# A four-layer conditional residual stack on one core: setup as movable stages with products of zeros, the last pair's adapter batch by batch with filler products, and tables of their own for two pairs at each end

## The chip, the core and the metric

The kernel runs on 1 core of one Trainium2 chip. The metric is the device time of one execution in microseconds (us); the kernel before takes 1067.29 us, the median of 3 runs (1067.28 to 1068.83). The engines are PE (TensorE: matrix products and transposes), DVE (VectorE), ACT (ScalarE), POOL (GpSimd) and SP (SyncE, which here issues nearly all DMAs). Each engine works through its own queue of instructions in order.

## What is computed

32 batches of 256 x 256 numbers go through four layers, each added to its input:

```python
x = x + attention(x, f, len)      # 16 heads of 16
x = x + adapter(x, language)
x = x + linear(x, subject)
x = x + pooling(x, prompt_type)
```

- Attention: queries are from `f + b_self`, keys and values from `x` (keys with `b_prev`), masked by a length for each batch, and each query also has its own key and value from `f`. In the reference:

```python
score_prev = einsum('bhqd,bhkd->bhqk', q, k[:, :, :l1]) * SCALE
score_self = (q * k[:, :, l1:]).sum(-1, keepdims=True) * SCALE
score_prev = where(mask, score_prev, -inf)
weights = softmax(concatenate([score_prev, score_self], -1))
attn = einsum('bhqk,bhkd->bhqd', weights[..., :-1], v[:, :, :l1])
attn = attn + weights[..., -1:] * v[:, :, l1:]
return attn @ Wo + bo
```

- Adapter: `relu(x @ W1[language] + b1) @ W2[language] + b2`, added to x and normalised (layernorm) with gamma and beta of the language. 256 to 64 to 256 columns.
- Linear: `x @ W[subject].T + b[subject]`.
- Pooling: `scores = tanh(x @ W1 + b1) @ v`; each of 256 rows takes a softmax of the scores under one of three masks (up to the row, from the row, all but the row), weighs the rows of x with it and divides by the count.

All is in float32.

## The kernel before

Two batches make a pair, 16 pairs in all. The work on a pair is cut into some 110 stages: small functions that take the pair's number p and mostly the batch within the pair (i) and issue a few instructions each. Every stage has a time in a table: FIRST for pair 0, SLOTS for pairs 1 to 14, LAST for pair 15, and ONCE for what is done once. A pair's times are shifted by PERIOD = 16 for each pair. At the end of the program all stages of all pairs are sorted by time and called in that order, so the tables alone fix the order in every engine's queue (the scheduler is switched off by `tc.manual_schedule()`). A pair's times run from about -14 to 55, so that some four pairs are under way together: while the scores of one pair are computed, the adapter, the linear layer and the pooling of earlier ones are done, and the loads of later ones.

The stages that matter here, with the lines of the profile:

- Beginning. A fixed head loads lengths, biases, Wq and Wk, makes masks and constants (`cols`, `len_f`, `mcol`, `ones`; zeroed buffers `vpad`, `nmpad`, `epad` on POOL) and two tiny products (cols_ps L640). `setup_q`, `setup_k`, `setup_ks` (L684) each do four products of one column with a weight to get a projected bias, and `setup_k` also loads Wv, Wo and others on ACT's queue, `setup_ks` the ids on SP's. `setup_rest` makes `heads`, `vbc` and the constant xconst (L737). For pair 0 xT is loaded on ACT's queue, everything else on SP's.
- Attention. proj_q, proj_k, proj_ks (L937: qps, kps, ksps, two products of 512 columns each); self_values and proj_v (vs_ps, v_ps, L804); s1 (L1036: scores s, eight products into a tile of four PSUM banks, of which there is one), row_max (L1049 on DVE), max_T (L1065) and max_own (L1073), which put the row maximum into the q tile by a DMA; s2 (L1145: the scores again, transposed, into the same tile), exps (L1157 on ACT), av (L1167); av_blocks, sums, weighted, with_own (L1179 to L1199, DVE and POOL), att_T (L1206), out_proj (o_ps, L804).
- Adapter. x_bias (L892, POOL) adds xconst to x; x1_out (L1222), x1_T; hidden (L1251: h_ps), h_out (L1265 on ACT: hT), adapted (L1279: y_ps), each for both batches of a pair at once; y_out (L1290), norm_stats (L1298), norm_rstd (L1306 on POOL), norm_shift, norm (L1320 on ACT), x2_out (L1328 and L1329 on DVE: multiply by gamma into x1c, add into x1b), x2_T (L786: transposes into x2T_ps).
- Linear and pooling. subject (z_ps, L804), x2_bias (L1342 on POOL), x3_out; pool_hidden (L1362: t_ps), th_out (L1376 on ACT), both for two batches at once; pool_scores (L1384), pool_mask (L1394), pool_exp (L1405), pr_T (L786), pooled (p_ps, L804), store (L1433).

The helper `product` (L804) does v, vs, o, z and p: four products of 256 columns each. PSUM has one tile of four banks for scores, one bank for av, and three tiles of 128x512 (`g_tile`) in turn for everything else.

Of the kernel before, what the change touches and what calls it, by code (L numbers as in the profile page):

```python
# [16 lines left out]
P = 128  # L17
# [19 lines left out]
    (("setup_q",), -49.3857),  # L37
    (("setup_k",), -19.8446),
    (("setup_ks",), -6.186),
    (("setup_rest",), -3.7537),  # L40
    (("setup_tw_bias",), 1.524),
    (("setup_tw_load", 0), 2.5417),
    (("setup_tw", 0), 5.9494),
    (("setup_tw_load", 2), 10.3657),
    (("setup_tw_load", 1), 11.2065),
    (("setup_tw", 1), 11.7201),
    (("setup_tw", 2), 12.0733),
    (("setup_tw_load", 3), 15.02),
    (("setup_tw", 3), 15.4506),
    (("setup_tw_load", 5), 17.2034),  # L50
    (("setup_tw_load", 4), 17.9245),
    (("setup_tw", 4), 21.0263),
    (("setup_tw", 5), 23.7521),
    (("setup_tw_load", 6), 24.1631),
    (("setup_tw_load", 7), 24.4783),
    (("setup_tw", 6), 26.9562),
    (("setup_tw", 7), 28.331),
    (("setup_pool",), 28.3669),
# [4 lines left out]
    (("load_T", "xT"), -13.5215),  # L63
    (("load_T", "fT"), -10.3917),
    (("key_mask", 0), -9.9073),
    (("mask_keys", 0), -7.2255),
    (("key_mask", 1), -4.9533),
    (("proj_q", 0), -4.4466),
    (("mask_keys", 1), -3.9573),
    (("q_out", 0), -3.6777),  # L70
    (("proj_k", 0), -2.4273),
    (("k_out", 0, 1), -1.9747),
    (("self_values", 0), -1.5169),
    (("k_out", 0, 0), -1.1613),
    (("vs_blocks", 0), -0.0939),
    (("proj_k", 1), 0.1938),
    (("s1", 0, 0), 0.9084),
    (("k_out", 1, 0), 1.2453),
    (("row_max", 0, 0), 1.3039),
    (("proj_q", 1), 1.586),  # L80
    (("k_out", 1, 1), 3.0678),
    (("s1", 0, 1), 3.244),
    (("q_out", 1), 3.2483),
    (("proj_ks", 0), 3.5014),
    (("row_max", 0, 1), 3.5842),
    (("ks_out", 0), 4.797),
    (("proj_v", 0), 5.2874),
    (("s1", 0, 2), 5.6623),
    (("row_max", 0, 2), 5.7692),
    (("proj_ks", 1), 5.795),  # L90
    (("spread_q", 1, 1), 5.8634),
    (("ks_out", 1), 5.8758),
    (("spread_q", 1, 0), 5.9303),
    (("s1", 0, 3), 7.7652),
    (("row_max", 0, 3), 7.7705),
    (("proj_v", 1), 8.095),
    (("spread_q", 0, 1), 8.1965),
    (("v_out", 0), 8.4638),
    (("v_out", 1), 8.8903),
    (("load_x",), 9.0442),  # L100
    (("s1", 1, 0), 9.0718),
    (("spread_q", 0, 0), 9.4749),
    (("ones_rows", 0), 9.491),
    (("own",), 9.7621),
    (("row_max", 1, 0), 9.8401),
    (("own_out",), 9.9648),
    (("load_adapter", 1), 10.5636),
    (("max_T", 0), 10.8193),
    (("s1", 1, 1), 11.1319),
    (("max_own", 0), 11.2444),  # L110
    (("row_max", 1, 1), 11.6016),
    (("s2", 0, 0), 11.6887),
    (("exps", 0, 0), 12.3045),
    (("s1", 1, 2), 13.3127),
    (("row_max", 1, 2), 14.1015),
    (("s2", 0, 1), 14.1573),
    (("exps", 0, 1), 14.4065),
    (("s1", 1, 3), 14.948),
    (("av", 0, 1), 15.0649),
    (("av", 0, 0), 15.0931),  # L120
    (("row_max", 1, 3), 15.3191),
    (("own_exp", 0), 15.5608),
    (("max_T", 1), 15.661),
    (("max_own", 1), 15.664),
    (("s2", 0, 2), 16.0157),
    (("exps", 0, 2), 16.2354),
    (("ones_rows", 1), 16.6823),
    (("av_blocks", 0, 0), 18.0554),
    (("own_blocks", 0), 18.3788),
    (("s2", 0, 3), 18.4335),  # L130
    (("own_exp", 1), 18.607),
    (("weighted", 0), 18.6408),
    (("av", 0, 2), 18.8873),
    (("exps", 0, 3), 18.9415),
    (("sums", 0, 0), 19.5731),
    (("s2", 1, 0), 20.565),
    (("with_own", 0, 0), 21.02),
    (("exps", 1, 0), 21.4915),
    (("av", 0, 3), 21.9185),
    (("s2", 1, 1), 22.6692),  # L140
    (("self_values", 1), 22.7919),
    (("exps", 1, 1), 23.02),
    (("av_blocks", 0, 1), 23.1327),
    (("sums", 0, 1), 23.5444),
    (("vs_blocks", 1), 23.6805),
    (("with_own", 0, 1), 23.7081),
    (("av", 1, 0), 23.7805),
    (("x_bias",), 24.2529),
    (("s2", 1, 2), 24.3639),
    (("att_T", 0), 24.4799),  # L150
    (("out_proj", 0), 24.5865),
    (("exps", 1, 2), 24.8801),
    (("x1_out", 0), 24.9932),
    (("load_adapter", 0), 25.6776),
    (("own_blocks", 1), 25.9991),
    (("av", 1, 1), 26.0785),
    (("av_blocks", 1, 0), 26.4561),
    (("s2", 1, 3), 26.6748),
    (("exps", 1, 3), 26.6765),
    (("weighted", 1), 26.9644),  # L160
    (("av", 1, 3), 27.5753),
    (("av", 1, 2), 27.5808),
    (("load_subject",), 27.9373),
    (("x1_T", 0), 28.0348),
    (("sums", 1, 0), 28.1731),
    (("with_own", 1, 0), 28.187),
    (("av_blocks", 1, 1), 28.6458),
    (("sums", 1, 1), 28.6986),
    (("with_own", 1, 1), 28.8383),
    (("x1T_out", 0), 29.2985),  # L170
    (("att_T", 1), 29.737),
    (("x1_b2", 0), 29.7867),
    (("out_proj", 1), 30.1273),
    (("x1_out", 1), 30.1913),
    (("x1_T", 1), 32.2936),
    (("x1T_out", 1), 32.4643),
    (("x1_beta", 0), 32.9228),
    (("x1_beta", 1), 33.8118),
    (("hidden",), 34.6069),
    (("h_out",), 35.0271),  # L180
    (("x1_b2", 1), 35.3287),
    (("adapted",), 36.3452),
    (("y_out", 1), 36.5305),
    (("y_out", 0), 36.6375),
    (("norm_stats", 0), 37.1251),
    (("norm_stats", 1), 37.201),
    (("norm_rstd", 0), 37.246),
    (("norm_rstd", 1), 37.2713),
    (("norm_shift", 0), 37.4371),
    (("norm", 0), 38.2498),  # L190
    (("norm_shift", 1), 38.2508),
    (("x2_out", 0), 39.0757),
    (("x2_T", 0), 39.6396),
    (("norm", 1), 39.7894),
    (("x2_bias", 0), 40.0974),
    (("x2_out", 1), 40.1578),
    (("x2T_out", 0), 40.3738),
    (("x2_T", 1), 40.4639),
    (("load_pool",), 40.7288),
    (("x2T_out", 1), 41.1509),  # L200
    (("pool_hidden",), 41.4167),
    (("th_out",), 41.5067),
    (("pool_scores", 0), 42.2295),
    (("x2_bias", 1), 42.4414),
    (("pool_scores", 1), 42.6152),
    (("pool_mask", 0), 42.7126),
    (("subject", 0), 42.9261),
    (("x3_out", 0), 43.2303),
    (("pool_mask", 1), 43.6816),
    (("pool_exp", 0), 44.056),  # L210
    (("subject", 1), 44.2113),
    (("pool_exp", 1), 44.3238),
    (("x3_out", 1), 44.7583),
    (("pr_T", 0), 46.893),
    (("prT_out", 0), 47.2894),
    (("pr_T", 1), 47.5751),
    (("pool_factor", 1), 47.6166),
    (("pool_factor", 0), 47.9292),
    (("prT_out", 1), 48.0167),
    (("pooled", 0), 49.1393),  # L220
    (("store", 0), 50.5365),
    (("pooled", 1), 53.4761),
    (("store", 1), 54.4432),
# [4 lines left out]
    (("load_T", "xT"), -37.5523),  # L228
    (("key_mask", 0), -19.5291),
    (("mask_keys", 0), -13.821),  # L230
    (("key_mask", 1), -12.6569),
    (("load_T", "fT"), -9.8489),
    (("mask_keys", 1), -7.5382),
    (("proj_k", 0), -5.9091),
    (("k_out", 0, 1), -5.8806),
    (("proj_q", 0), -2.9721),
    (("k_out", 0, 0), -2.808),
    (("self_values", 0), -2.1146),
    (("q_out", 0), -1.6303),
    (("s1", 0, 0), -0.879),  # L240
    (("proj_k", 1), 0.1292),
    (("row_max", 0, 0), 0.8243),
    (("k_out", 1, 0), 0.9903),
    (("k_out", 1, 1), 1.4355),
    (("s1", 0, 1), 1.5728),
    (("proj_q", 1), 1.6701),
    (("spread_q", 0, 1), 2.6443),
    (("proj_ks", 0), 3.2664),
    (("row_max", 0, 1), 3.4033),
    (("q_out", 1), 3.476),  # L250
    (("s1", 0, 2), 3.7112),
    (("spread_q", 1, 1), 4.0254),
    (("proj_ks", 1), 4.6937),
    (("ks_out", 0), 5.0527),
    (("row_max", 0, 2), 5.6196),
    (("ks_out", 1), 5.8464),
    (("spread_q", 0, 0), 6.0284),
    (("vs_blocks", 0), 6.3593),
    (("s1", 0, 3), 7.2806),
    (("own",), 7.3892),  # L260
    (("proj_v", 0), 7.4415),
    (("row_max", 0, 3), 7.549),
    (("spread_q", 1, 0), 7.7204),
    (("s1", 1, 0), 7.7777),
    (("max_T", 0), 7.7783),
    (("own_out",), 10.1669),
# [290 lines left out]
def cond_resid_kernel(  # L557
# [41 lines left out]
    def g_tile(name):  # L599
        return ps_g.tile([P, 512], F32, tag="g", name=name)  # L600
# [943 lines left out]
```

## Time and profile before

| | |
|---|---|
| median of 3 runs | 1067.29 us |
| the profiled execution | 1068.81 us |
| its span | 1066.7 us |
| mean granted TensorE clock | 0.995 |
| DVE, ACT, POOL busy | 70%, 48%, 34% |
| PE busy in the first 10 us / the next 10 | 2.16 / 8.88 us |
| PE busy from 1040 to 1050 us / 1050 to the end | 5.15 / 11.92 us |
| granted clock in those two | 0.80 / 0.81 |
| time from one pair to the next (pairs 3 to 13) | 63.6 us |

A row of the profile reads: start, duration (both in us), engine, line, operation, output <- inputs, and in brackets how long the engine had stood idle before it and what released it. In a table of waits it is: engine, tile and line of the waiting instruction <- engine, tile and line of the one waited for: total us, times, longest. In a table of windows: the window's length, then busy time of PE, PEld (weight loads), DVE, ACT and POOL (with the number of instructions), the granted clock, the DMA share, GB/s.

### The profile page before, as it was taken

How to read it: one execution, taken by the hardware profiler on the slowest of the kernel's cores; microseconds unless marked ns; L12 is line 12 of the kernel's file. 1: busy time of each engine (PE TensorE's matmuls, PEld its weight loads, DVE VectorE, ACT ScalarE, POOL GpSimd, SP SyncE). 2: the span in 40 equal slices, each digit the busy share in tenths (PEclk: the TensorE clock that was granted, in tenths of full speed). 3: DMA queues.
4: the chain of work that ended last, by engine and by line, in shares of the span. 5: the costliest groups of instructions: out<-in, count | busy, mean ns of one | idle time of the engine just before them, and what ended most of it. 6: DMA issues, size and time to landing. Idle time of an engine off the chain costs nothing.

```text
span 1066.7 us, 20863 instructions
## 1 busy us (share of the span) xinstructions
PE 1029.1 (96%) x7912; PEld 591.9 (55%) x7912; DVE 750.7 (70%) x1239; ACT 514.1 (48%) x722; POOL 367.5 (34%) x489
## 2 busy tenths in 40 slices
PE   6999999999999999999999999999999999999996
PEld 4455555555555555555555555555555555555564
DVE  4757586767768687686767867686786867757764
ACT  1243454544545544545545545455455545455552
POOL 2022362432424244233332514243233333514541
PEclk9999999999999999999999999999999999999998
DMA  4223231321313132132311312222132311311222
GB/s 136 60 71 104 84 105 49 106 59 53 115 64 91 39 99 76 53 91 67 98 50 62 111 57 91 58 84 74 52 96 70 103 57 56 101 34 52 68 76 68
DMA packets 58985, 81.08 MB, mean 76 GB/s; under 512 B 7238, under 2 KB 40774, under 8 KB 58886
## 3 DMA queue, kind: packets, MB, share of 16 engines
q1 hardware_dynamic: 57782, 77.46, 24.4%
q10 hardware_dynamic: 864, 1.51, 0.6%
q8 instruction: 63, 1.03, 0.4%
q0 software_dynamic: 240, 0.79, 0.2%
q14 instruction: 36, 0.29, 0.1%
HBM read 68.45 MB, written 9.71 MB: 73 GB/s over the span
## 4 chain that ended last, share of the span: by engine, by line
PE 86%; DVE 9%; ACT 2%; POOL 1%; DMA 1%; issue 1%; SPq 0%; DVEq 0%; ACTq 0%
PE s L1036 13%; PE s L1145 11%; PE av L1167 10%; PE kps L937 6%; PE z_ps L804 5%; PE ksps L937 5%; PE o_ps L804 5%; PE qps L937 5%; PE p_ps L804 5%; PE vs_ps L804 5%; DVE nmpad L1049 4%; PE v_ps L804 3%; DVE x1c L1328 2%; PE t_ps L1362 2%; PE y_ps L1279 2%; PE x2T_ps L786 2%
## 5 line engine op out<-in xcount | busy, mean ns | idle before, releaser
L1157 ACT ACTIVATE e<-s 128x2048 f32<-128x2048 f32 x128 | 240.3, 1878 | 377.5 <-PE s L1145 377.5
L1049 DVE TENSOR_REDUCE nmpad<-s 128x8 f32<-128x2048 f32 x128 | 292.7, 2287 | 164.6 <-PE s L1036 164.6
L1036 PE MATMUL s<-k,qc 32*128 32x512 f32 x1024 | 146.0, 640 | 4.1 <-ACT e L1157 2.8
L1145 PE MATMUL s<-q,k 32*128 32x256 f32 x2048 | 146.7, 400 | 1.4 <-DVE nmpad L1049 1.2
L1132 POOL TENSOR_TENSOR vs<-vs,eown 128x256 f32<-128x256 f32 x64 | 38.9, 629 | 292.4 <-DVE eown L1097 292.4
L1167 PE MATMUL av<-e,vpad 128*32 128x256 f32 x2048 | 130.7, 383 | 0.0
L1145 PEld LDWEIGHTS s<-q,k 32*128 32x128 f32 x2048 | 92.5, 184 | 51.7 <-issue 20.6
L1167 PEld LDWEIGHTS av<-e,vpad 128*32 128x32 f32 x2048 | 57.8, 109 | 83.6 <-issue 42.5
L1198 POOL TENSOR_TENSOR vs<-bt,vs 128x256 f32<-128x256 f32 x64 | 46.9, 733 | 111.3 <-DVE bt L1179 111.3
L1199 POOL TENSOR_TENSOR vs<-vs,zs 128x256 f32<-128x256 f32 x64 | 40.3, 630 | 108.0 <-DVE zs L1189 104.4
L964 ACT ACTIVATE k<-kps,kbias,cols 128x512 f32<-128x512 f32 x64 | 49.4, 777 | 53.3 <-PE kps L937 53.0
L937 PE MATMUL kps<-xT,wks 128*128 128x512 f32 x128 | 65.0, 632 | 1.1 <-issue 1.1
L804 PE MATMUL v_ps<-wvs,xT 128*128 128x256 f32 x256 | 63.7, 392 | 0.0
L1036 PEld LDWEIGHTS s<-k,qc 32*128 32x128 f32 x1024 | 40.0, 183 | 42.6 <-ACT e L1157 24.9
L804 PE MATMUL vs_ps<-fT,wvs 128*128 128x256 f32 x256 | 63.6, 391 | 0.0
L937 PE MATMUL ksps<-fT,wks 128*128 128x512 f32 x128 | 63.4, 618 | 0.0
L804 PE MATMUL z_ps<-ws,x2T 128*128 128x256 f32 x256 | 62.7, 389 | 0.0
L937 PE MATMUL qps<-fT,wqs 128*128 128x512 f32 x128 | 62.0, 607 | 0.0
L804 PE MATMUL o_ps<-wos,attT 128*128 128x256 f32 x256 | 61.8, 384 | 0.1
L804 PE MATMUL p_ps<-x2b,prT 128*128 128x256 f32 x256 | 61.8, 385 | 0.0
L804 PEld LDWEIGHTS p_ps<-x2b,prT 128*128 128x128 f32 x256 | 47.3, 190 | 16.5 <-issue 10.0
L804 PEld LDWEIGHTS o_ps<-wos,attT 128*128 128x128 f32 x256 | 47.2, 190 | 16.5 <-issue 10.4
(130 smaller groups left out, 1489.2 us busy)
## 6 DMA issues: line engine op xcount, KB each, us to landing
an<-in_adn SPq DMA_DIRECT2D x32, 384.0 KB
mk<-pool_d SPq DMA_DIRECT2D x32, 257.0 KB
fT<-in_fT SPq DMA_DIRECT2D x16, 512.0 KB
xs<-in_x SPq DMA_DIRECT2D x32, 256.0 KB
ws<-in_swT SPq DMA_DIRECT2D x32, 256.0 KB
out<-x2b SPq DMA_DIRECT2D x32, 256.0 KB
xT<-in_xT SPq DMA_DIRECT2D x15, 512.0 KB
wb<-in_sb SPq DMA_DIRECT2D x32, 128.0 KB
```

Of the source, the lines that this page charges most:

```text
L786: nc.tensor.transpose(ps[:, cc, q * P : (q + 1) * P], src[:, q, cc * P : (cc + 1) * P], ident,)
L804: nc.tensor.matmul(ps[:, q, :n], lhsT=lhsT(c, q), rhs=rhs[:, c, :], start=(c == 0), stop=(c == 1),)
L937: nc.tensor.matmul(ps, lhsT=w[:, ci, c * P : (c + 1) * P], rhs=T[src, p][:, ci].rearrange("p b s -> p (b s)"), start=(ci == 0), stop=(ci = ...
L964: nc.scalar.activation(joint("k", p, work, [P, 2, 2, 2, S])[:, u, c].rearrange("p b s -> p (b s)"), T["kps", p, c], AF.Identity, bias=kbia ...
L1036: nc.tensor.matmul(ps[:, j], lhsT=T["qc", p][r, c, i, q * P : (q + 1) * P], rhs=T["k", p][r, :, c, i, :], start=True, stop=True,)
L1049: nc.vector.tensor_reduce(nm_bufs[i][:, q, g : g + 8].rearrange("p (u j) -> p j u", u=2), T.pop(("s1", b, n)), AX.X, ALU.max, negate=True,)
L1132: nc.gpsimd.tensor_tensor(vs, vs, e.unsqueeze(3).to_broadcast([P, S // HB, 2, DH]), ALU.mult)
L1145: nc.tensor.matmul(ps[:, j, k, :], lhsT=T["k", p][r, u, c, i, k * P : (k + 1) * P], rhs=T["q", p][r, u, c, i, :], start=True, stop=True,)
L1157: nc.scalar.activation(e, T.pop(("s2", b, n)), AF.Exp)
L1167: nc.tensor.matmul(ps[j * HB : (j + 1) * HB, u, :], lhsT=v_bufs[b % 3][:, k, 8 * c + 2 * j + u, :], rhs=e[:, j, k, :], start=(k == 0), sto ...
L1198: nc.gpsimd.tensor_tensor(vs, bt[:, :, :, 0:DH], vs, ALU.add)
L1199: nc.gpsimd.tensor_tensor(vs, vs, z.unsqueeze(3).to_broadcast([P, S // HB, 2, DH]), ALU.mult)
```

## The change

Five things are done.

1. Loads of weights and ids, and len_f, mcol, ones, heads, vbc and xconst, become stages of their own in ONCE. Wk's load goes behind ACT's table load, Wv, Wo and the rest move from ACT's queue to SP's. epad's memset becomes the first work of POOL.
2. `setup_warm`: three stages of two products of zeros each. Two come after cols_ps, one after bq_ps.
3. hidden, h_out, adapted, pool_hidden and th_out may take one batch; LAST uses this, the other tables don't.
4. `keep_warm`: four stages in LAST of two products each, the result of which is not used.
5. The tables: all are made anew, SECOND (pair 1) and NEXT_TO_LAST (pair 14) are added. In SLOTS (now pairs 2 to 13) x_bias goes from 24.25 to 13.93, ahead of the second s2; load_x from 9.04 to 2.94; load_pool from 40.73 to 38.30; proj_ks of the second half goes behind the fourth s1. On PE the out_proj of a second batch now comes before the x2_T of the second batch of an earlier pair, where it was behind it. In FIRST proj_q comes before proj_k and load_x, x_bias and the ids' users are placed otherwise.

```diff
+    def setup_load(name):
+        nc_, t_, src = {
+            "wq": (nc.sync, wqs, wq),
+            "wk": (nc.scalar, wks, wk),
+            "wv": (nc.sync, wvs, wv),
...
+        }[name]
+        nc_.dma_start(out=t_, in_=src)
+
+    epad = const.tile([P, S], F32, name="epad")
+    nc.gpsimd.memset(epad, 0.0)
...
+    def setup_warm(n):
+        ps = g_tile(f"warm{n}")[:, 0:S]
+        for _ in range(2):
+            nc.tensor.matmul(ps, lhsT=epad[:, 0:P], rhs=epad, start=True, stop=True)
...
-        for t_, w in ((wvs, wv), (wos, wo), (pws, pw)):
-            nc.scalar.dma_start(out=t_, in_=w)
-        nc.scalar.dma_start(out=xconst, in_=bo.to_broadcast([P, D]))
...
-    def hidden(p):
-        ps = g_tile(f"h_ps{p}")[:, 0:S]
+    def hidden(p, *which):
+        which = which or (0, 1)
+        ps = g_tile(f"h_ps{2 * p + which[0]}")[:, 0:S]
         for c in range(2):
-            for i in range(2):
+            for i in which:
...
+    def keep_warm(p, n):
+        ps = g_tile(f"keep{n}")[:, 0:D]
+        for _ in range(2):
+            nc.tensor.matmul(ps, lhsT=ident, rhs=wqs[:, 0, :], start=True, stop=True)
...
-        table = FIRST if p == 0 else LAST if p == NP - 1 else SLOTS
+        table = {0: FIRST, 1: SECOND, NP - 2: NEXT_TO_LAST, NP - 1: LAST}.get(p, SLOTS)
```

The beginning in ONCE, and the places in SLOTS and LAST that the text speaks of:

```diff
-    (("setup_q",), -49.3857),
-    (("setup_k",), -19.8446),
-    (("setup_ks",), -6.186),
-    (("setup_rest",), -3.7537),
+    (("setup_warm", 2), -106.0922),
+    (("setup_load", "wq"), -75.9765),
+    (("setup_load", "lang"), -72.4551),
+    (("setup_load", "wk"), -70.4394),
+    (("setup_warm", 0), -67.4191),
+    (("setup_len",), -53.0448),
+    (("setup_q",), -51.9044),
...
+    (("setup_warm", 1), -25.0685),
+    (("setup_load", "wo"), -23.0732),
+    (("setup_ks",), -19.1134),
...
+    (("setup_k",), -14.712),
...
-    (("x_bias",), 24.2529),
+    (("x_bias",), 13.9304),
...
-    (("x2_out", 0), 39.0757),
-    (("x2_T", 0), 39.6396),
+    (("x2_out", 0), 39.0849),
+    (("x2_T", 0), 39.3257),
...
-    (("x2_T", 1), 40.4639),
+    (("x2_T", 1), 40.9718),
...
+    (("keep_warm", 2), 22.9284),
...
+    (("hidden", 0), 31.3764),
...
+    (("hidden", 1), 34.0171),
...
+    (("adapted", 1), 35.466),
+    (("keep_warm", 0), 35.5617),
...
+    (("keep_warm", 3), 39.523),
...
+    (("keep_warm", 1), 42.895),
+    (("x2_T", 0), 43.4213),
...
+    (("pool_hidden", 1), 47.0899),
+    (("pool_hidden", 0), 47.2477),
```

## The prediction

> **What bounds the kernel now.** I read the page's busy shares first, then PE's waits, then windows of one pair, and last the two ends row by row.
>
> ```profile
> PE 1029.1 (96%) x7912; PEld 591.9 (55%) x7912; DVE 750.7 (70%) x1239; ACT 514.1 (48%) x722; POOL 367.5 (34%) x489
> ```
>
> PE is busy for 1029.1 of 1066.7 us. No product of the work is removed, so all that can be won is 1066.7 - 1029.1 = 37.6 us of idle time and the products that ran at half clock. Who takes the idle time is in PE's waits (total, times, longest):
>
> ```profile
> PE x2T_ps L786 <- DVE x1b L1329: 17.0, 15, 4.2
> PE bq_ps L684 <- DMA wqs<-in_wq: 6.4, 1, 6.4
> PE s L1036 <- ACT e L1157: 2.8, 4, 1.1
> ```
>
> The first row is 10.3 us in 11 waits between 200 and 900 us, and it is PE's only wait there. The windows of one pair (63.6 us; PE's busy time comes first) say the same: 63.60 - 62.69 = 0.91 us idle in each.
>
> ```profile
> 252.30:315.90 63.60, 62.69 (x490) 35.87 (x489) 46.46 (x74) 32.00 (x46) 22.30 (x30) 1.00 0.25 75
> 888.40:952.00 63.60, 61.98 (x480) 35.57 (x484) 45.48 (x72) 32.52 (x47) 22.18 (x28) 1.00 0.22 65
> ```
>
> The timeline of one pair shows where it comes from:
>
> ```profile
> 461.53 2.36 POOL L892 TENSOR_TENSOR xs<-xs,xconst 128x1024 f32<-128x1024 f32 x1
> 462.70 1.73 DVE L1328 TENSOR_TENSOR x1c<-x1c,an 128x512 f32<-128x512 f32 x1
> 464.47 0.72 DVE L1329 TENSOR_TENSOR x1b<-x1b,x1c 128x512 f32<-128x512 f32 x1
> 465.34 0.63 PE L786 MATMUL x2T_ps<-ident,x1b 128*128 128x128 f32 x4 [0.91 <-DVE x1b L1329]
> ```
>
> The multiplication of L1328 takes 1.73 us beside POOL's 2.36 us x_bias, and 0.70 us elsewhere. Those 1.0 us are PE's 0.91. The slowing is of DVE work within SBUF: a row maximum that reads PSUM takes 2.25 us at 484.79 beside POOL's L1228, as always.
>
> The end, from PE's timeline:
>
> ```profile
> 1045.25 0.63 PE L786 MATMUL x2T_ps<-ident,x1b 128*128 128x128 f32 x4 [4.15 <-DVE x1b L1329]
> 1046.58 1.09 PE L786 MATMUL x2T_ps<-ident,x1b 128*128 128x128 f32 x4 [0.70 <-DVE x1b L1329]
> 1047.60 2.77 PE L1362 MATMUL t_ps<-x2T,tw 128*64 128x256 f32 x8
> 1050.93 1.71 PE L1384 MATMUL sc_ps<-th,vbc 64*128 64x256 f32 x4 [0.56 <-ACT th L1376]
> 1052.57 3.75 PE L804 MATMUL z_ps<-ws,x2T 128*128 128x256 f32 x8
> ```
>
> PE runs out of work at 1041.1 and waits for the layernorm of the last pair; then its clock is at half. The window 1046 to 1056 us shows a granted clock of 0.50.
>
> The beginning:
>
> ```profile
> 8.85 1.84 PE L684 MATMUL bq_ps<-bcols_in,wqs 128*128 128x1 f32 x8 [6.42 <-DMA wqs<-in_wq]
> ...
> 15.22 3.58 PE L937 MATMUL kps<-xT,wks 128*128 128x512 f32 x4 [1.12 <-issue]
> 18.64 1.03 PE L737 MATMUL xc_ps<-wos,bvw 128*128 128x256 f32 x4
> 19.50 1.88 PE L937 MATMUL qps<-fT,wqs 128*128 128x512 f32 x4
> ```
>
> kps takes 3.58 us where the equal qps takes 1.88: the clock is at half until 18.50 us.
>
> **The middle (pairs 2 to 13; nothing added or removed).** x_bias goes from 24.25 to 13.93 in SLOTS, a stretch in which DVE mostly reduces scores out of PSUM, and on PE out_proj of the second batch now comes before its x2_T. So the first thing removed is 0.91 x 11 = 10.0 us (10.3 by the waits row); pair 14 has a table of its own, and its window had 63.6 - 61.98 = 1.62 us idle and the one after it 0.93, of which I count 1. What is late next: I walked the new PE order of one pair by the rows' start-to-start times (S products 1.07, projections 1.9, v, vs, o, z and p 1.83, av 1.0, h 1.01, y 1.07, x2T 0.55) and found PE at the second x2_T at 30.9 us after the pair's S1 of the first batch, its input ready at 29.95. The thinnest margins are 0.05 to 0.4 us (score products behind the exponentials), 0.2 (y behind hT) and 0.4 (z behind the pooling mask). Moves of loads (load_x 9.04 to 2.94, load_pool 40.7 to 38.3) lie on SP, with a DMA share of 0.25, and lead their users by tens of us. If x_bias slows the work that it now lies beside, that is max_own and sums: 1.0 us each, of which I let at most 0.5 a pair reach PE, as DVE is idle 63.6 - 46.5 = 17 us in a pair. **Middle: -11; bounds -12.8 (all its idle time) and -5 (0.5 us a pair given back).**
>
> **The head.** Removed: wks and xT no longer lead ACT's queue, the table load does; the small copies of setup_rest and len_f, mcol and ones go where later work needs them; epad's memset (0.31 us) becomes POOL's first work. Added: six products of zeros of 256 columns. One such product is 1.83 / 4 = 0.46 us at full clock by the z rows and 3.68 / 4 = 0.92 by the cold z, 0.86 by kps's 3.42 / 4. Two pairs come right after cols, at 2.5 us, and last 3.44 us, in the 6.42 us that PE waits for wqs (cover: 8.71 - 2.5 = 6.2 us, so they are free); the third, 0.9 to 1.7 us, lies behind bq on the path. DMAs: SP now issues len_i, bcols, wqs, ids, fT0, wos, ids, adapter rows, and later wvs; fT0 waits for len_i (landed 6.2 us before), so it lands at 8.5 to 11, where it landed before 9.98. Value loads and wvs are behind it in SP's queue and are used after the first S products. New chain: wqs at 6 to 8.7, bq, warm1, bks, bk (1.75 us each cold, by bq's row, 0.9 warm), qps, kps, xc. If the clock is full from about 6 us on, these three are done at 14.5 instead of 21.38: -6 to -7. If it is not until a dense window after the tiny products, bq to bk end near 13.1, qps takes 3.4 cold, and the gain is 0.6 to 2.3. The rows on the clock: it rose after 15.1 to 18.5 (97% busy) and after 1052.75 to 1056.16; its steps are whole multiples of 3.413 us apart (1027.41 = 301 of them), so it looks at a grid, and the grid's line nearest below 2.5 us is at 1.43. The window 1.43 to 4.85 would be about 70% dense, and one that was 85% busy with half-array products (1049.3 to 1052.75) did not raise it. **Head: -4, midway; bounds +1 (warm1 cold on the path and fT0 at 11) and -7.**
>
> The Trainium skill (TensorE: Matmul & The Clock Gate, Part 1) says that the clock rises after one busy window of about 3.4 us in a grid that runs on whatever the kernel does. That speaks against this part: 3.44 us of zeros hold a whole window only if they begin with it. By the rule alone the head would be -1.5 and the whole gain 2.5 us smaller. The grid in the rows above agrees with it; how busy is busy enough, no row shows.
>
> **Pairs 0 and 1** were idle 1.96 us between 20 and 61.5 and 3.09 in the next 63.6 us, 5.05 in all. Walked in the new order, the first 50 us wait 2.7 us (S2 behind its row maxima 0.5 and 0.55, a score product behind the exponential 1.1, and small ones). **-1; bounds -3 and +2.**
>
> **The tail.** Moved: hidden, h_out and adapted of batch 30 no longer wait for batch 31, so its layernorm chain (1038.8 to 1045.2 before) starts some 2 us earlier; z and p of pair 14 are kept to fill PE while it runs. Added: four stages of two products, 8 x 0.43 = 3.45 us, one before the last scores are done (0.86), three in the gap. From the end of the last S2 (1023.16 before) to the end of p I add: o, t, x2T, x1T, z, h and y to 12.35, 1.2 idle for the last batch's hT behind exponentials on ACT, filler, prT, z, two fillers and x2T of batch 30 to 19, p of pair 14 with x2T of 31 to 22.8, then t 1.0, sc 0.9, z 1.7, prT 0.55, z 1.8, prT 0.55, p 3.5: 32.8 us against 1062.51 - 1023.16 = 39.35. From that gain 0.86 goes for the filler ahead of this stretch, and something for x2T and t of pair 14, which moved into it from before and so won elsewhere. A check by sums: idle 4.15 + 0.70 + 0.56 + 0.56 = 5.9, half-clock price (t 1.7, sc 1.0, z 1.8, x2T 0.5) 5.0, together 10.9, less 3.45 of filler: 7.4. **Tail: -6.5; bounds -8 and -3** (clock kept, but the fillers' 3.45 stand in the way of ready work).
>
> **Sum.** -11 - 4 - 1 - 6.5 = -22.5. From the profiled execution's 1068.81 us (span 1066.7 and 2.1 around it): 1046.3. The other two runs are 1.5 us below it, so the median can lie at 1045; I say 1046.
>
> **Rivals.** A change of under 0.2% (2.1 us) can't be told from none here.
> - The fillers don't hold the clock. For: a window 18% busy dropped it, and the fillers leave gaps at hT and the norm. Against: three fillers and two z and p lie between y and x2T. Price: half clock again over one to three windows, 5.0 in the tail, and the head's case of -1: 1046.3 + 4.5 + 3 = 1054.
> - The middle's wait only moves: out_proj now stands first and waits for att_T, or z for its mask. For: margins of 0.2 to 0.4 us. Against: the 17 us of DVE idle. Then 11 us are not won: 1057.
> - Slower: x_bias at 13.93 slows max_own or the SBUF operations around it, the nmT rows reach q late, and S2 waits at PE in each of 12 pairs. From 1068.81 - 11.5 = 1057.3, the point of no change is 11.5 / 12 = 0.96 us a pair; two operations slowed by 1.0 us with no slack give 2 x 12 = 24 more: 1081. For: L1328's row. Against: max_own reads PSUM.
> - The head works in full and the tail too: 1041, which is in the first case's own range.
>
> **Chances.** Forecast (1041 to 1051) 0.56; fillers fail 0.22; the wait moves 0.12; new wait over 1.2 us a pair 0.06; between them, no change, 0.04. Faster by over 0.2%: 0.56 + 0.22 + 0.12 = 0.90; within: 0.04; slower: 0.06. The range 1040 to 1056 holds the first two cases nearly whole, 0.8.
>
> **What would show it.** The middle: no x2T row in PE's waits between 200 and 900 us, 62.7 us from one pair to the next, and L1328 at 0.70 us throughout. The head: the granted clock full before 9 us, and qps, kps, xc done near 14.5 (clock raised) or 19 to 21 (not raised). The tail: granted clock 1.00 to the last product and t, sc, z at 1.0, 0.7, 1.9 us. A row such as S L1145 behind nmpad with 12 or more waits would prove the forecast wrong.

## The result and the profile after

The changed kernel takes 1057.38 us (median of 4 runs, 1056.18 to 1057.54) against 1068.04 before in the same comparison: a ratio of 0.9898, 95% interval 0.9881 to 0.9915. It is faster by 10.7 us, about half of the 22.5 that were forecast, and above the range of 1041 to 1051. Its profiled execution took 1057.54 us, span 1055.7.

The page's busy row and PE's waits (all of 1.3 us and more) of the changed kernel:

```profile
PE 1035.9 (98%) x7940; PEld 599.9 (57%) x7940; DVE 738.6 (70%) x1239; ACT 515.5 (49%) x722; POOL 361.9 (34%) x489
```

```profile
PE bq_ps L1061 <- DMA wqs<-in_wq: 2.5, 1, 2.5
PE s L1521 <- DVE nmpad L1425: 2.4, 5, 0.6
PE o_ps L1180 <- DVE pnmx L1775: 1.8, 1, 1.8
PE cols_ps L1008 <- DVE rows L1005: 1.4, 1, 1.4
PE x2T_ps L1162 <- DVE x2b L1729: 1.3, 1, 1.3
```

The row of 17.0 us is gone, and PE's idle time fell from 37.6 to 1055.7 - 1035.9 = 19.8 us: 17.8 less. But PE is busy for 6.8 us more, and 17.8 - 6.8 = 11.0 us is the change of the span. The zeros and fillers, the split products and products at half clock in the head are in those 6.8 us; the half clock of the tail went out of them.

A window of the changed kernel shows the middle (columns as before):

```profile
313.20:375.90 62.70, 62.70 (x491) 36.16 (x490) 44.92 (x77) 32.02 (x45) 22.04 (x30) 1.00 0.24 76
```

From 250.5 to 877.5 us every window of 62.70 us is 62.70 us busy: the 0.91 us a pair are gone. The two windows ahead of them are not full: 1.96 us idle from 125.1 to 187.8, and 0.77 in the next. The width of a window is not the time of a pair: from the first row maximum of pair 5 to that of pair 13 (DVE, L1049 before, L1425 after) there are 508.82 us before and 499.77 after, so a pair takes 63.60 and 62.47 us. It gains 1.13, more than its 0.91 of idle time, because PE's busy time for the same 3905 records of products fell too, from 501.57 to 499.77. One place where that shows is behind the wait: x2T, 0.53 us from its start to the next start elsewhere, took 0.62 there.

The head, in PE's timeline of the changed kernel:

```profile
2.35 3.78 PE L1051 MATMUL warm<-epad 128*128 128x256 f32 x8
8.63 1.84 PE L1061 MATMUL bq_ps<-bcols_in,wqs 128*128 128x1 f32 x8 [2.49 <-DMA wqs<-in_wq]
10.32 2.05 PE L1051 MATMUL warm<-epad 128*128 128x256 f32 x4
...
15.45 3.76 PE L1313 MATMUL qps<-fT,wqs 128*128 128x512 f32 x4
19.00 3.10 PE L1313 MATMUL kps<-xT,wks 128*128 128x512 f32 x4
...
22.80 1.88 PE L1313 MATMUL ksps<-fT,wks 128*128 128x512 f32 x4
```

All of qps and most of kps run at half clock (3.55 us from start to start, against 1.8 later). The next product starts at 22.80; in the kernel before, the one behind the same three started at 21.22. So the head lost 1.6 us. The page prints a granted clock of 1.00 for these first 20 us, as it did before: here the record has no event of the clock until it rises, and the durations alone show the half clock.

The tail, in PE's timeline of the changed kernel:

```profile
1023.25 1.08 PE L1628 MATMUL h_ps<-x1T,a 128*64 128x256 f32 x4
...
1025.47 1.13 PE L1654 MATMUL y_ps<-a,hT 64*128 64x256 f32 x4
1026.53 1.08 PE L1628 MATMUL h_ps<-x1T,a 128*64 128x256 f32 x4
1028.17 1.13 PE L1654 MATMUL y_ps<-a,hT 64*128 64x256 f32 x4 [0.56 <-ACT hT L1643]
...
1036.07 0.66 PE L1162 MATMUL x2T_ps<-ident,x1b 128*128 128x128 f32 x4 [1.33 <-DVE x2b L1729]
```

In the middle, where h and y are still done for two batches at once, the same timeline has:

```profile
440.50 1.08 PE L1628 MATMUL h_ps<-x1T,a 128*64 128x256 f32 x8
...
443.64 1.14 PE L1654 MATMUL y_ps<-a,hT 64*128 64x256 f32 x8
```

Four products of one batch take as long as eight of two batches (h 1.08 and 1.08, y 1.13 and 1.14): split, h and y of a pair take 2 us more than joined in the middle. And x2T waits for x3_out, not for its own input.

The time by stretches, between marks that are the same work in both kernels: the first row maximum of pair 0 (24.31 us before, 25.89 after) and of pair 4 (245.64, 247.97), the end of the last s2 (the next product starts at 1023.16 and 1014.24), and the end of the span.

| stretch | before | after | difference | moved work put back | forecast |
|---|---|---|---|---|---|
| head, to pair 0 | 24.31 | 25.89 | +1.6 | +1.6 | -4 |
| pairs 0 to 3 | 221.33 | 222.08 | +0.75 | +0.75 | -1 (pairs 0 and 1) |
| middle, to the last s2 | 777.52 | 766.27 | -11.25 | -10.3 | -11 |
| tail | 43.54 | 41.46 | -2.1 | -3.1 | -6.5 |
| sum | 1066.7 | 1055.7 | -11.0 | -11.0 | -22.5 |

The fifth column puts two things where the forecast had them: x2T and t of pair 14 (2.03 us), which moved from ahead of the last s2 to behind it, are counted in the middle, and the filler ahead of the last s2 (1.06) in the tail.

### The profile page after: what moved, and what is told of

It reads as the page before. It is cut to its first block, busy times and chain, and to the rows that moved or that the text cites. A ratio compares the mean times of both kernels' runs of the same rounds, so it can differ in the third digit from the quotient of the medians.

```text
span 1055.7 us, 20836 instructions
## 1 busy us (share of the span) xinstructions
PE 1035.9 (98%) x7940; PEld 599.9 (57%) x7940; DVE 738.6 (70%) x1239; ACT 515.5 (49%) x722; POOL 361.9 (34%) x489
## 4 chain that ended last, share of the span: by engine, by line
PE 92%; DVE 3%; ACT 3%; DMA 1%; issue 1%; POOL 0%; SPq 0%; DVEq 0%; ACTq 0%; POOLq 0%
PE s L1521 13%; PE s L1412 13%; PE av L1543 11%; PE ksps L1313 6%; PE v_ps L1180 5%; PE qps L1313 5%; PE o_ps L1180 5%; PE p_ps L1180 5%; PE vs_ps L1180 5%; PE kps L1313 5%; PE z_ps L1180 5%; ACT e L1533 2%; PE y_ps L1654 2%; PE h_ps L1628 2%; PE t_ps L1737 2%; PE x1T_ps L1162 2%
## 5 line engine op out<-in xcount | busy, mean ns | idle before, releaser
L1425 DVE TENSOR_REDUCE nmpad<-s 128x8 f32<-128x2048 f32 x128 | 293.2, 2290 | 173.1 <-PE s L1412 172.7
L1313 PE MATMUL qps<-fT,wqs 128*128 128x512 f32 x128 | 65.1, 632 | 0.0
L1180 PE MATMUL o_ps<-wos,attT 128*128 128x256 f32 x256 | 62.7, 388 | 2.4 <-DVE pnmx L1775 1.8
L1340 ACT ACTIVATE k<-kps,kbias,cols 128x512 f32<-128x512 f32 x64 | 46.9, 782 | 30.7 <-PE kps L1313 30.5
L1180 PEld LDWEIGHTS vs_ps<-fT,wvs 128*128 128x128 f32 x256 | 46.1, 189 | 20.9 <-issue 12.6
L1680 POOL TENSOR_SCALAR rstd<-mv 128x2 f32<-128x2 f32 x32 | 7.9, 248 | 142.3 <-DVE mv L1673 142.3
```

Source lines behind the costliest of these rows:

```text
L1180: nc.tensor.matmul(ps[:, q, :n], lhsT=lhsT(c, q), rhs=rhs[:, c, :], start=(c == 0), stop=(c == 1),)
L1313: nc.tensor.matmul(ps, lhsT=w[:, ci, c * P : (c + 1) * P], rhs=T[src, p][:, ci].rearrange("p b s -> p (b s)"), start=(ci == 0), stop=(ci = ...
L1340: nc.scalar.activation(joint("k", p, work, [P, 2, 2, 2, S])[:, u, c].rearrange("p b s -> p (b s)"), T["kps", p, c], AF.Identity, bias=kbia ...
L1425: nc.vector.tensor_reduce(nm_bufs[i][:, q, g : g + 8].rearrange("p (u j) -> p j u", u=2), T.pop(("s1", b, n)), AX.X, ALU.max, negate=True,)
```

## The experiments

Medians of 4 runs each (e7: 10), with the kernel before on the same chip at 1067.2 to 1067.9 (1068.04 in the comparison above). Ratios are to that; a difference of under 1 us between two experiments is within what the chips differ by. Loads and constants as stages, SECOND and NEXT_TO_LAST were not tried alone.

**e1: no products of zeros.**

```diff
-    (("setup_warm", 2), -106.0922),
-    (("setup_warm", 0), -67.4191),
-    (("setup_warm", 1), -25.0685),
```

> The changed kernel without its three stages of products of zeros; nothing else differs. Theory: the first two stages lie in the wait for wqs and raise no clock, and the third (1.85 us at half clock) stands on the path ahead of qps; without it the first products start 1.8 us earlier, a full window of the clock's grid is dense one window earlier in most executions, and the time is 2 to 4 us less than the changed kernel's 1057.4 (1053.5 to 1055.5). Rival: the zeros do help the clock; then the first products run at half clock for longer and the time is the same or 1 to 3 us more.

1054.91 us (ratio 0.9879, 0.9863 to 0.9896). The rows of e1:

```profile
13.97 3.61 PE L1310 MATMUL qps<-fT,wqs 128*128 128x512 f32 x4
17.42 1.88 PE L1310 MATMUL kps<-xT,wks 128*128 128x512 f32 x4
```

qps starts 1.5 us earlier and kps runs at full clock, so that S1 starts at 21.81 instead of 24.61 (23.04 in the kernel before, so the rest of the new head is worth 1.2 us here). The products of zeros, as the change has them, are a loss.

**e2: zeros twice as long in the wait, none behind bq.**

```diff
-    (("setup_warm", 1), -25.0685),
...
-        for _ in range(2):
+        for _ in range(4):
             nc.tensor.matmul(ps, lhsT=epad[:, 0:P], rhs=epad, start=True, stop=True)
```

> The changed kernel with the first two stages of zeros twice as long (eight products, 6.9 us at half clock, from 2.35 us to past the landing of wqs) and without the third. Theory: a whole window of 3.4 us is now dense whatever the grid's phase, so the clock rises before 8 us; warm rows (0.43 us for two records) appear among the zeros. If it then holds over the 24 one-column products, qps and kps take 1.7 us each and the time is 5 to 7 us less than the changed kernel's 1057.4; if it drops, 1 to 3 us less. Rival: products of zeros do not raise the clock at all: zeros at half clock to the end at 9.2 us, and the time 1 to 2 us less, by the third stage alone.

1052.34 us (0.9860, 0.9844 to 0.9877). The timeline of e2:

```profile
2.35 5.94 PE L1050 MATMUL warm<-epad 128*128 128x256 f32 x16
8.77 1.02 PE L1060 MATMUL bq_ps<-bcols_in,wqs 128*128 128x1 f32 x8 [0.47 <-DMA wqs<-in_wq]
...
11.44 1.96 PE L1312 MATMUL qps<-fT,wqs 128*128 128x512 f32 x4
```

Zeros do raise the clock: 16 records take 5.94 us where half clock would take 16 x 0.43 = 6.9, bq takes 1.02 instead of 1.84, and S1 starts at 18.60. What the changed kernel's zeros lacked is length: 3.78 us of them did not raise it.

**e3: x_bias alone, in the kernel before.**

```diff
-    (("x_bias",), 24.2529),
+    (("x_bias",), 13.9304),
```

> The kernel before with one number of its table SLOTS changed: x_bias at 13.93 instead of 24.25. Theory: this alone takes POOL's 128x1024 operation away from L1328, which takes 0.70 us throughout; PE's wait of x2T behind x1b goes, and the period of a pair falls from 63.6 to 62.7 us: 10 to 12 us less than before (1056 to 1058). Rival: the order on PE (out_proj ahead of the second x2_T) is what removed the wait; then the period stays at 63.2 to 63.6 and the time within 4 us of before.

1055.76 us (0.9892, 0.9876 to 0.9909): one number takes as much as the whole change. From pair 5 to pair 13 a pair takes 62.53 us. A window of e3:

```profile
315.00:377.70 62.70, 62.70 (x493) 35.91 (x489) 45.41 (x74) 32.18 (x46) 21.84 (x29) 1.00 0.25 76
```

Its four runs lie at 1053.6, 1054.2 and twice at 1057.4. The profile is of a 1053.6 one, and in it the clock was at half for 6.8 us of the tail; in that of the kernel before it was for 10.2. How the clock's steps fall may thus be part of the spread of these runs; that is not shown.

**e4: no filler in the tail.** The four keep_warm lines of LAST are left out.

> The changed kernel without its four filler stages in the last pair. Theory: they cost their 3.5 us of PE and hold a tile of PSUM each, and the wait for the layernorm is short enough now that the clock holds without them: PE busy 3.4 us less, idle 1 to 2 us more, time 1 to 2.5 us less than 1057.4. Rival: without them the clock drops to half for at least one window in the tail, as in the kernel before, and the time is 2 to 5 us more.

1060.31 us (0.9929, 0.9913 to 0.9946): 2.9 more than the changed kernel: the rival was right. The timeline of e4:

```profile
1036.52 3.75 PE L1176 MATMUL p_ps<-x2b,prT 128*128 128x256 f32 x8 [1.78 <-DVE x2b L1725]
```

Waits of 1.60 and 1.78 us with one short group between them are enough: this p runs at half clock. In this tail the fillers earn their place.

**e5: hidden, h_out and adapted of the last pair for both batches at once.**

```diff
-    (("hidden", 0), 31.3764),
...
-    (("hidden", 1), 34.0171),
+    (("hidden",), 34.0171),
```

> The changed kernel with hidden, h_out and adapted of the last pair for both batches at once again (at the places of the second batch), y_out, norm_stats and norm_rstd of the first batch right behind; nothing else. Theory: the two batches' products lie on different halves of the array and run side by side, so splitting them has cost 1.0 us in h and 1.0 in y; joined, PE's busy time falls by 2 us, but the first batch's layernorm starts about 2 us later and PE waits longer for the first x2_T: time between 1 us less and 1 more than 1057.4. Rival: split and joined take the same time on PE; then only the delay shows, and the time is 2 us more.

1058.55 us (0.9912, 0.9896 to 0.9929), 1.2 more, though the intervals overlap. PE is busy 1035.4 us, only 0.5 less. Joined at this place, h takes 1.88 us (from 1024.43 to 1026.31) and y 1.55, together 3.43 and not the 2.08 of the middle, as h waits inside for x1T of the second batch; the four split groups take 4.14. PE has new waits of 1.50 us (a filler behind ACT's prT) and 0.90 (p behind x3_out). So here splitting costs some 0.7 us of PE, not the 2 of the expectation, and returns more.

**e6: x3_out of batch 29 earlier.**

```diff
-    (("x3_out", 1), 56.7429),
+    (("x3_out", 1), 55.0),
```

> The changed kernel with one number changed: x3_out of batch 29 at 55.0 instead of 56.74 in NEXT_TO_LAST, ahead of the norm_shift of batch 31 in DVE's queue. Theory: the 1.3 us in which PE waits for x2T of batch 30 are not the layernorm (x1b was ready 2 us before) but the z tile of PSUM, which x3_out frees, and x3_out stands behind a norm_shift that waits for POOL; with it ahead, the wait is gone and the time 1.0 to 1.4 us less. Rival: the wait is the layernorm's; then nothing changes.

1056.97 us (0.9897, 0.9880 to 0.9913): no gain that can be told. The wait moved. The timeline of e6:

```profile
1034.52 0.60 PE L1162 MATMUL x2T_ps<-ident,x1b 128*128 128x128 f32 x4
1034.96 1.89 PE L1180 MATMUL p_ps<-x2b,prT 128*128 128x256 f32 x8
1038.17 0.63 PE L1162 MATMUL x2T_ps<-ident,x1b 128*128 128x128 f32 x4 [1.32 <-DVE pz L1794]
```

The first x2T no longer waits for its tile, but the second now waits the same 1.3 us. DVE's pz comes right behind the x1b that it needs.

**e7: LAST of the kernel before for pair 15, SLOTS for pair 14.**

> The changed kernel with the table LAST of the kernel before for the last pair and SLOTS for the one before it: no filler, both batches at once. What the new tail is worth. By the sums of the trace the new tail gained 2.5 to 3 us (idle 5.9 and half clock 5.0 before; idle 2.9, filler 3.45 and split 2.0 after), so this should be 1059.5 to 1060.5, with the clock at half for one to three windows. Rival (as in the prediction): the new tail gained 6.5, and this is 1063 or more.

1070.48 us (1.003, 1.002 to 1.004). Worse than either expected, and not a measure of the tail: an old table beside new ones makes seams (S waits 2.4 us for a row maximum, nm_ps 1.7, vs_ps 2.5). The clock dropped behind two of them: it was 0.83 from 930 to 940 and from 980 to 990 us. Its record also has 0.74 in the first 20 us, where its tables are those of the changed kernel. Tables that were made for their neighbours can't be exchanged one by one.

**e8: e2 and e6 together.**

> The changed kernel with both edits that have won or should: two stages of zeros of twice the length without the third, and x3_out of batch 29 at 55.0. If the two are independent: 5.0 and 1.2 us less than 1057.4, so 1051.

1052.30 us (0.9855, 0.9838 to 0.9871): e2's gain and nothing from e6. In this execution the clock rose among the zeros, as in e2, but fell again behind the one-column products. The windows of e8, clock in the third column from the end:

```profile
9.00:12.00 3.00, 3.00 (x25) 2.77 (x25) 1.96 (x14) 0.00 (x0) 0.00 (x0) 1.00 0.58 171
12.00:15.00 3.00, 3.00 (x5) 1.23 (x4) 2.88 (x13) 0.00 (x0) 0.93 (x1) 0.51 1.01 222
```

**e9: e6, and x1_beta of batch 31 ahead of its norm_rstd on POOL.**

```diff
-    (("x1_beta", 1), 40.9688),
+    (("x1_beta", 1), 36.6),
```

> e6 (x3_out of batch 29 at 55.0) with x1_beta of batch 31 at 36.6 instead of 40.97 in LAST, so that on POOL it comes before the norm_rstd of batch 31. In e6 PE waits 1.3 us for x2T of batch 31; its norm_shift took 1.22 us (0.17 in the kernel before) beside POOL's x1_beta. Theory: the layernorm of batch 31 is slowed by that neighbour; with it gone norm_shift takes 0.2 us, the wait falls to 0.1 to 0.4 us and the time is 0.9 to 1.2 us less than e6 (1056.97), so 1055.9. Rival: the wait is the chain's own length; then the wait stays at 1.0 us or more.

1055.20 us (0.9889, 0.9872 to 0.9905), 1.8 less than e6. The norm_shift in the changed kernel, and then in e9:

```profile
1034.20 1.21 DVE L1686 SCALAR_TENSOR_TENSOR rstd<-mv,rstd 128x2 f32<-128x2 f32 x1 [0.60 <-POOL rstd L1681]
```

```profile
1033.08 0.16 DVE L1686 SCALAR_TENSOR_TENSOR rstd<-mv,rstd 128x2 f32<-128x2 f32 x1
...
1035.97 0.63 PE L1162 MATMUL x2T_ps<-ident,x1b 128*128 128x128 f32 x4 [0.18 <-DVE pz L1794]
```

Two numbers a row took 1.21 us beside POOL's x1_beta and 0.16 without it. It is the same slowing as in the middle, on the chain that x2T waits for. The other slow step of that chain stays in e9 (1.20 us at 1031.85), since its neighbour is another, DVE's x2_out of batch 30. In the changed kernel, where DVE's L1703 runs from 1032.91 to 1033.60:

```profile
1032.97 1.20 POOL L1681 TENSOR_TENSOR rstd<-rstd,mhalf 128x2 f32<-128x2 f32 x1
```

It takes 0.71 us in the kernel before. The profile of e9 also shows the clock at the head, with the changed kernel's own zeros, which e9 leaves as they are:

```profile
9.20:9.30 0.10, 0.10 (x3) 0.10 (x2) 0.00 (x0) 0.00 (x0) 0.00 (x0) 0.61 0.95 328
...
9.30:15.00 5.70, 5.70 (x25) 5.34 (x24) 3.42 (x19) 0.00 (x0) 0.43 (x1) 0.50 0.75 224
...
19.40:19.60 0.20, 0.20 (x2) 0.07 (x1) 0.20 (x1) 0.00 (x0) 0.00 (x0) 0.84 1.09 326
```

The clock falls at 9.22 us, inside bq, and rises again at 19.46: it is at half for 10.24 us, three times 3.41. That it had been up ahead of 9.22 the rows of bq show (1.43 us for eight, between 1.02 at full clock and 1.84 at half). If it was up for one step of 3.41, it rose near 5.8, in the last of the zeros; that is an estimate. With luck the short zeros raise the clock; it has fallen again before qps, after PE's wait of 2.7 us for wqs.

**e10: x_bias put back to 24.25 in the changed kernel's SLOTS.**

> The changed kernel with x_bias in SLOTS put back to 24.25 (pairs 2 to 13); nothing else. Theory: the slow L1328 comes back, but in the new order out_proj of the second batch stands before the second x2_T, so that part of the 1.0 us is covered. If the order covers none of it: 0.9 us in each of 11 or 12 pairs, 1067 to 1069, no better than the kernel before. If it covers all: 1057 to 1058. I take the first, because e3 got the whole gain without the order.

1054.95 us (0.9882, 0.9866 to 0.9899). A miss: nothing comes back, the middle's windows stay full, a pair takes 62.47 us as in the changed kernel, and the time is 2.4 less. The new order alone covers the slow L1328 (L1702 in this kernel, 1.30 us at 461.02). PE's waits between 30 and 250 us sum to 4.3 us instead of 6.0, which is 1.7 of the 2.4. The largest part, 1.1, is at 168 us, where PE's o_ps waits for a pooling mask. DVE in the changed kernel, then in e10:

```profile
165.71 2.22 DVE L1254 COPY_PREDICATED xT<-off,first 128x512 f32<-128x512 int32 x1
```

```profile
165.66 1.15 DVE L1254 COPY_PREDICATED xT<-off,first 128x512 f32<-128x512 int32 x1
```

x_bias, where the change put it, runs beside this mask_keys (POOL from 165.00, 2.35 us), and the wait behind it is 1.83 us instead of 0.74. (0.74 us is also what such a row takes with no neighbour, in e14 at 460.88; the 1.15 of e10 has POOL's x2_bias beside it.)

**e11: e8 and e9's edit.**

> e8 (zeros of twice the length, x3_out at 55.0) with x1_beta of batch 31 at 36.6. If e9's edit wins 1.0 us, 1051.3; without that 1052.3.

1050.82 us (0.9845, 0.9828 to 0.9861): as expected, 1.5 less than e8.

**e12: the kernel before with three edits.** x_bias as in e3, eight products of zeros behind cols_ps, and in LAST one stage of eight fillers:

```diff
+    (("keep_warm",), 37.6),
     (("x2_T", 0), 38.5295),
...
+        if p == NP - 2:
+            table = [(s, 53.55 if s == ("store", 1) else at) for s, at in table]
```

> The kernel before with three edits and none of the new tables: x_bias at 13.93 in SLOTS (as e3), eight products of zeros behind cols_ps, and one stage of eight filler products behind the last p of pair 14, in PE's 4.15 us gap (store of batch 29 at 53.55, so that its PSUM tile is free in time). Theory: the last pair loses little by its order and much by the clock: the fillers lie wholly in the gap and the half clock (5.0 us by the rows of the kernel before, less where the grid falls well) goes; the zeros save 1.5 to 2.5 us. From e3's 1053.6 to 1057.4: 1049 to 1052, as fast as or faster than the best so far. Rival: the fillers push the last x2T back, or the clock drops all the same; then 1053 or more.

1057.24 us (0.9904, 0.9888 to 0.9921): a miss, of my own making. The moved store's DMA came ahead of load_subject on SP, and SP stood at it from 1020.88 for 8 us. The loads behind it came late, PE waited 3.8 us for tw (1.45 and 2.36), and the clock dropped to 0.50 from 1040 to 1045 us.

**e13: e12 with the loads ahead of the store.**

```diff
-    (("load_subject",), 37.7733),
+    (("load_subject",), 37.40),
-    (("load_pool",), 38.4068),
+    (("load_pool",), 37.45),
```

> e12 with load_subject and load_pool of the last pair at 37.40 and 37.45, ahead of the moved store in SP's queue, so that the 3.8 us wait of t_ps for tw goes. Theory: the old tail order loses by its half clock, not by its order: 3.8 us less than e12 and the half clock's 3 to 5 us kept off, 1050 to 1053 after e12's 1057.2. Rival: the gap of the layernorm shows again or the clock drops all the same: 1054 or more, and the new tail's batch by batch order is worth its cost.

1050.34 us (0.9843, 0.9826 to 0.9859). The tail of e13:

```profile
1025.06 3.62 PE L1389 MATMUL keep<-wqs,ident 128*128 128x256 f32 x16
1029.38 0.63 PE L791 MATMUL x2T_ps<-ident,x1b 128*128 128x128 f32 x4 [0.70 <-DVE x1b L1334]
...
1032.01 1.08 PE L1367 MATMUL t_ps<-x2T,tw 128*64 128x256 f32 x6 [0.15 <-ACT x2T L800]
```

The layernorm of the last pair is as long as before, the fillers lie wholly in PE's gap, and t, sc and z run at full clock. Without any of the new tables this is 7 us faster than the change by the medians, some 6 by the ratios.

**e14: the order alone, in the kernel before.**

```diff
-    (("att_T", 0), 24.4799),
+    (("att_T", 0), 24.10),
-    (("x2_T", 1), 40.4639),
+    (("x2_T", 1), 40.62),
```

> The kernel before with two numbers changed in SLOTS: x2_T of the second batch at 40.62 (behind out_proj of the first batch of the pair after next, 24.5865) and att_T of the first batch at 24.10 (ahead of x2_out on DVE). x_bias stays at 24.25. Theory from e10: L1328 stays slow (1.3 to 1.7 us) and costs nothing, because o_ps's 1.83 us now lie ahead of the transposes that wait for it; the period falls to 62.7 and the time to 1055 to 1058, as e3. Rival: x_bias must move (or other moves of the new table are needed): period 63.2 or more, 1062 or more.

1053.55 us (0.9868, 0.9852 to 0.9885). The timeline of e14:

```profile
457.30 2.35 POOL L892 TENSOR_TENSOR xs<-xs,xconst 128x1024 f32<-128x1024 f32 x1
458.48 0.70 DVE L1206 STREAM_TRANSPOSE attT<-vs 128x512 f32<-128x512 f32 x1
459.11 1.10 DVE L1328 TENSOR_TENSOR x1c<-x1c,an 128x512 f32<-128x512 f32 x1
460.14 1.99 PE L804 MATMUL o_ps<-wos,attT 128*128 128x256 f32 x8
460.24 0.72 DVE L1329 TENSOR_TENSOR x1b<-x1b,x1c 128x512 f32<-128x512 f32 x1
461.97 0.60 PE L786 MATMUL x2T_ps<-ident,x1b 128*128 128x128 f32 x4
```

x1b ends at 460.96, o_ps keeps PE until 461.97. The multiplication is still slowed, and PE no longer waits for it: a pair takes 62.47 us. The edit changes the order in two queues, PE's and, with att_T, DVE's; neither was tried without the other.

**e15: e11 with x_bias back at 24.25.**

> e11 (zeros of twice the length without the third stage, x3_out at 55.0, x1_beta of batch 31 at 36.6) with x_bias back at 24.25 in SLOTS as in e10. If e10's 2 us are no chance: 1048.5 to 1049.5; if they are: 1050.8.

1049.50 us (0.9839, 0.9822 to 0.9855), the fastest of all; its interval overlaps that of e13.

## Why the prediction missed

Right in kind and nearly in size: **the middle**. The forecast was -11, measured -10.3 with the moved work put back (62.47 us a pair, where the prediction named 62.7), and no new wait opened between 250 and 877 us: the rival that the wait only moves (1057) named the right time for the wrong reason. The reason given, x_bias leaving L1328's side, is sufficient (e3) but not necessary: the order of out_proj and x2_T, which the prediction named and gave no share, does the same with the place of att_T (e14), and with the new tables x_bias might have stayed (e10). That out_proj is of the first batch of a pair (24.88 in SLOTS), not of the second as the text on the change and the prediction have it.

Wrong, by 5.6 us: **"Head: -4, midway"**. The midpoint stood for nothing. The trace allowed the two cases, the worked grid (first window 70% dense) and the rule of TensorE: Matmul & The Clock Gate (Part 1 of the page in the Trainium skill) both spoke for the low one, and I took a value between that no execution could show. The low case itself was sized too well: its 13.1 us for the end of bk needs wqs near 6 us, the early end of the 6 to 8.7 that the prediction gave. bq started at 8.63, bk ended at 15.45, the third stage of zeros cost its 1.85 us in full, and the clock stayed at half through qps and most of kps. e1 (2.5 us less without zeros) and e2 (5.0 less with zeros long enough) settle it. What e9 shows agrees with the rule's grid: half clock for three steps of 3.41 us.

Wrong, by 3.4 us: **"Tail: -6.5"**. The stretch that the prediction put at 32.8 us, from the end of the last s2 to the end of p, took 37.1 (1014.24 to 1051.36). Two steps of the walk failed. The first put h and y of one batch at half the time of two. The products from the last s2 to the second y, which it added up to 12.35, take 14.43 (1014.24 to 1029.23, less 0.56 of waiting), 2.1 us more. The second left x2T of batch 30 without a wait; PE waited 1.33 us for it. Its PSUM tile is freed by x3_out, which stood in DVE's queue behind norm_shift of batch 31, and that was late twice: POOL's two steps ahead of it took 0.76 and 1.20 us instead of 0.22 and 0.71 beside DVE's x2_out, and norm_shift itself 1.21 instead of 0.16 beside POOL's x1_beta. e6 shows that the place of x3_out alone only moves the wait, e9 that with x1_beta away it falls to 0.18. The rest is smaller: 0.5 for th, and the pieces between the second y and x2T, which add up to about 0.5 more than the 19 that the prediction wrote. That the fillers hold the clock was right (e4), and so the rival of 1054, the fillers failing, was wrong.

Wrong, by 1.75 us: **the first pairs, at -1**. In the windows that the prediction walked, 20 to 125 us, PE's idle time fell by 0.7 (4.39 instead of 5.05), nearly as forecast. It rose in the two windows behind them, from 1.48 to 2.73, which no term of the prediction priced: there x_bias in its new place slows mask_keys (e10, and again e15, 1.3 us less than e11). That was the mechanism of the slower rival, at one place instead of twelve.

Open: the last 0.7 us by which e10 is faster than the changed kernel; how much of the differences of 1 us between runs is the phase of the clock's grid, which no kernel here controls; and where the 0.22 us of busy time a pair went, beyond the products right behind the wait.

## What to carry to other kernels

A stall that repeats in every period has two cures, take the slow neighbour away or put ready work in front of it, and one line of a table may be all that a large change is worth; try that line alone. Products that only hold the clock belong in a gap where the engine waits anyway (3.62 us of them in e13). Products that are to raise it must last well over one step of its grid, here 3.41 us, and have no long wait behind them: 5.94 us of zeros did in e2, while in e9 the clock fell again over a wait of 2.7 us. Where a moved step issues a DMA, look at what stands behind it in that queue: e12 lost 7 us by one store.

## What the runs showed of the hardware

- Products of zeros raise the clock as others do (e2, within 5.94 us). 24 one-column products behind them may let it fall (e8) or not (e2); whether the phase of the grid of 3.41 us decides it is not shown.
- Two products on different halves of the array, with 64 columns or 64 rows each, run side by side: eight take 1.08 us (h) and 1.14 (y), four 1.08 and 1.13.
- DVE work within SBUF is held up by a POOL operation beside it however small it is: 128x2 numbers took 1.21 us instead of 0.16 and ended at 1035.41, as POOL's x1_beta did (1034.14 + 1.26 = 1035.40). SBUF — State Buffer in the Trainium skill (SBUF: two separate sides) has it that a DVE instruction with two SBUF inputs and a POOL instruction that reads SBUF exclude each other for the whole instruction. These ends agree, and that norm_shift had two SBUF inputs. The price is what is left of POOL's instruction when DVE's starts, less about 0.15 us:

| DVE's row | left of POOL's | DVE alone | beside it | longer by |
|---|---|---|---|---|
| norm_shift, 1034.20, changed kernel | 1.20 | 0.16 | 1.21 | 1.05 |
| L1328, 462.70, kernel before | 1.19 | 0.69 | 1.73 | 1.04 |
| L1328, 459.11, e14 | 0.54 | 0.69 | 1.10 | 0.41 |
| mask_keys, 165.71, changed kernel | 1.64 | 0.74 | 2.22 | 1.48 |

The prediction priced every such meeting at 1.0 us, from the second row alone.
- It works the other way too: POOL's L1681 started at 1032.97 beside DVE's L1703, of which 0.63 us were left, and took 1.20 us instead of 0.71, 0.49 longer.
